# A fused attention, gated-convolution and axial-attention block on one core: the projection stored in four blocks, and three buffers for the local responses

## The chip, the cores and the metric

The kernel runs on one core of one Trainium2 chip. The metric is device time in microseconds (us) of one execution. The engines have short names throughout: PE is the matrix engine (PEld its weight load), DVE the vector engine, ACT the scalar engine, POOL the general-purpose engine, SP the engine that only issues transfers. SP's and POOL's transfers run on the same 16 DMA engines. L12 means line 12 of the kernel before.

## The reference, cut to what matters

Input and output are fp32 images of shape 4 x 64 x 256 x 256. Layer 0 works on them in this order:

```
xn   = channel_layernorm(x)
proj = conv1x1(xn, in_proj)                  # 64 channels
local, glob = proj[:, :32], proj[:, 32:]
local = gated 1x1 branch on local            # pre (1x1), a sigmoid response, a threshold = mean response
qkv  = depthwise3x3(conv1x1(glob))           # 96 channels
out  = top-k attention over channels (q, k, v), one small matrix per image
x    = x + conv1x1(concat(out, local), out_proj)
x    = x + gated convolution feed-forward(x) # 1x1 to 256 channels, depthwise 3x3 and 5x5, gelu gate, 8x8 FFT scaling
```

Layer 1 then does attention along rows, attention along columns and a feed-forward of width 256. Everything is fp32.

Two facts matter here. The response threshold needs the mean over the whole image, and the attention matrix needs sums over the whole image, so the projection has to be kept in DRAM and read again. And once an image's attention matrix is known, `v`, the attention, its scaling and the output projection collapse into one 3x3 convolution of `glob` to 64 channels, plus the local part.

## The kernel before

The work goes in five stages, each a Python loop that is fully unrolled. A scheduler places the recorded instructions: it fixes one order per engine ahead of time, and each engine then runs its own list in order and waits on semaphores. So an instruction that waits holds back everything behind it on its engine, needed or not.

**Stage A** (`stage_a`) goes over 4 images x 16 strips of 16 rows, 64 steps in all. `norm` normalises a strip. `proj` projects it to `pj`, 128 partitions of 2 branches x 2 row parities x 32 channels; partitions 0 to 63 are local and 64 to 127 global. `proj` ends with the stores of `pj` into `projd` in DRAM on POOL's queue, one per branch and parity (L551). Three steps behind, `pairs` builds the padded tile `gp` from `pj` by SBUF-to-SBUF transfers, clears its border columns on POOL (L569, L570), multiplies it into query/key tiles (L599), copies those out on DVE (`qT`, L604) and accumulates their Gram matrix (L590). For images 1 to 3, every second step also runs `local` for the image before: it reads `L4` from `projd` (L438), computes `pre` and a response `sw`, and stores them as `pred` and `resd`. After the loop, `local_last` does this for the last image while `attention_weights` makes the convolution weights `wc`.

**Stage C1** (`stage_c1`) goes over 32 strips of 8 rows x 2 pairs of images, 64 steps. `load` fetches, on SP's queue, `pre` (L718), `resp` (L719), two `gp` tiles (L725, L727, L729) and the input `xs` (L736). A `gp` tile here has 128 partitions: 32 global channels one row up, the same 32 unshifted, 32 local channels, and the 32 global ones one row down. The projection is stored once, so a tile takes three transfers:

```python
SY.dma_start(gp[32:96], pg[:, 8 * s:8 * s + 8])
SY.dma_start(gp[0:32, lo:8], pg[0:32, 8 * s - 1 + lo:8 * s + 7])
SY.dma_start(gp[96:128, 0:hi], pg[0:32, 8 * s + 1:8 * s + 1 + hi])
```

`front` turns the response into a mask in place (L743, then times `pre`, L744), runs the convolution in two halves of 24 matmul records each (L755) with the mask's matmul behind each half (L759), adds `xs` into `xm` (L765), transposes `xm` into `xmp` and normalises it. `back` transposes the normalised tile into `xl`. `hidden` makes the feed-forward's first 1x1 (L804), copies it out alternately on ACT (L810) and DVE (L808) into `tb`, and stores `tb` as `td` from POOL. All PSUM tiles of these steps rotate through six banks.

**Stage C2** does the depthwise convolutions, **C3** the FFT scaling and row attention, **D** the column attention and last feed-forward.

Of the kernel before, what the change touches and what calls it, by code (L numbers as in the profile page):

```python
# [9 lines left out]
F32 = mybir.dt.float32  # L10
# [4 lines left out]
C, H, W = 64, 256, 256  # L15
HW = H * W
# [231 lines left out]
def kernel(ctx: ExitStack, tc: tile.TileContext, x, packs, fd, out, off):  # L248
    nc = tc.nc
    B = x.shape[0]  # L250
    V, S, T, G, SY = nc.vector, nc.scalar, nc.tensor, nc.gpsimd, nc.sync
# [3 lines left out]
    dram = ctx.enter_context(tc.tile_pool(name="dram", bufs=1, space=bass.MemoryType.DRAM))  # L255

    def mm():
        return ps.tile([128, 512], F32, tag="mm", name="mm")
# [18 lines left out]
    V.memset(eps_t, EPS)  # L277


    projd = dram.tile([B, 64, H, W], F32, name="projd")  # L280


    NI, R0 = 9, 28
# [36 lines left out]
    p = sp1.enter_context(tc.tile_pool(name="pst", bufs=2))  # L320
# [113 lines left out]
    def local_load(b, i):  # L434
        l4 = p.tile([128, 8 * W], F32, name="L4")
        for k in range(4):
            r = 64 * k + 8 * i
            SY.dma_start(l4[k * 32:(k + 1) * 32], projd[b, 32:64, r:r + 8, :].rearrange("c u w -> c (u w)"))  # L438
        l4s[b, i] = l4

    def local_store(dst, b, i, src):
# [39 lines left out]
    def stage_a():  # L481
        NS = H // 16
        with tc.tile_pool(name="pa", bufs=2) as pa, tc.tile_pool(name="pa1", bufs=1) as pk:
# [4 lines left out]
            t = mm()  # L488
# [34 lines left out]
            def proj(b, s):  # L523

                pj = pa.tile([128, 8, W], F32, name="pj", bufs=4)
                pjs[b, s] = pj
                xn2 = xns.pop((b, s))
                xTs = []
                for hf in (0, 1):
                    xT = pa.tile([128, 1024], F32, name="xT")  # L530
                    for k in (0, 1):
                        tq = mm()
                        for i in range(4):
                            g = k * 8 + i * 2
                            T.transpose(tq[:, i * 128:(i + 1) * 128], xn2[hf][:, g:g + 2, :].rearrange("p a c -> p (a c)"), ident)
                        V.tensor_copy(xT[:, k * 512:(k + 1) * 512], tq)
                    xTs.append(xT)
                    yield
                for hf in (0, 1):
                    for k in (0, 1):  # L540
                        pr = mm()
                        T.matmul(pr, win, xTs[hf][:, k * 512:(k + 1) * 512], start=True, stop=True)
                        n = (s * 2 + hf) * 2 + k
                        S.activation(pj[:, hf * 4 + k * 2:hf * 4 + k * 2 + 2, :].rearrange("p a c -> p (a c)"), pr, AF.Identity,
                                     bias=bin_, accum_out=sacc[b][:, n:n + 1])
                    yield
                pv = projd[b, :, 16 * s:16 * s + 16, :].rearrange("(l c) (t a) w -> l a c t w", l=2, a=2)
                for lg in (0, 1):
                    for par in (0, 1):
                        q = lg * 64 + par * 32  # L550
                        G.dma_start(pv[1 - lg, par], pj[q:q + 32])  # L551
                hp = mm()
                for i in range(4):
                    T.matmul(hp[i * 32:(i + 1) * 32, :], K("g1T"), pj[:, 2 * i:2 * i + 2, :].rearrange("p a c -> p (a c)"), start=True, stop=True)
                hs = pa.tile([128, 512], F32, name="hs")
                V.tensor_scalar(hs, hp, K("g1b"), 0.0, ALU.add, ALU.max)
                hss[b, s] = hs
# [54 lines left out]
            for n in range(len(seq) + 3):  # L612
                if n + 1 < len(seq):
                    ld[seq[n + 1]] = load(*seq[n + 1])
                if 0 <= n - 2 < len(seq):
                    gate(*seq[n - 2])

                m = n - NS - 2
                lb, li = m // NS, m % NS
                if m >= 0 and lb < B - 1 and li % 2 == 0:  # L620
                    local_load(lb, li // 2)
                _steps(*(f(*seq[n - d]) for d, f in ((3, pairs), (1, proj), (0, norm)) if 0 <= n - d < len(seq)),
                       local(lb, li // 2) if m >= 0 and lb < B - 1 and li % 2 == 1 else None)
                if m >= 0 and lb < B - 1 and li == NS - 1:
                    local_end(lb)
                if n >= 1 and n - 1 < len(seq) and seq[n - 1][1] == NS - 1:
                    b = seq[n - 1][0]
                    V.tensor_reduce(sumA[:, b:b + 1], sacc[b], AX.X, ALU.add)
                    local_weights(b)
                if n >= 3 and seq[n - 3][1] == NS - 1:  # L630
                    b = seq[n - 3][0]
                    V.tensor_copy(gram2[b][0:64], grams[b][0:64, 0:64])
                    V.tensor_copy(gram2[b][64:128], grams[b][64:128, 64:128])
# [3 lines left out]
    def local_last():  # L637
        b = B - 1
        local_load(b, 0)
        for i in range(8):  # L640
            if i < 7:
                local_load(b, i + 1)
            yield from local(b, i)
        local_end(b)
# [49 lines left out]
    def stage_c1():  # L694
        NS = H // 8
        with ExitStack() as cs:
            p = cs.enter_context(tc.tile_pool(name="pc", bufs=2))
# [3 lines left out]
            t = mm()  # L701
# [6 lines left out]
            t = mm()  # L708
# [5 lines left out]

            def load(pr, s):
                pre = p.tile([128, 4 * W], F32, name="pre")
                resp = p.tile([128, 4 * W], F32, name="resp")
                SY.dma_start(pre, pred[pr, s].rearrange("h b c n -> (h b c) n"))  # L718
                SY.dma_start(resp, resd[pr, s].rearrange("h b c n -> (h b c) n"))  # L719
                gps = []  # L720
                for i in (0, 1):

                    gp = p.tile([128, 8, W], F32, tag="gp", name="gp", bufs=4)
                    pg = projd[2 * pr + i]
                    SY.dma_start(gp[32:96], pg[:, 8 * s:8 * s + 8])  # L725
                    lo = 1 if s == 0 else 0
                    SY.dma_start(gp[0:32, lo:8], pg[0:32, 8 * s - 1 + lo:8 * s + 7])  # L727
                    hi = 7 if s == NS - 1 else 8
                    SY.dma_start(gp[96:128, 0:hi], pg[0:32, 8 * s + 1:8 * s + 1 + hi])  # L729
                    if lo:  # L730
                        G.memset(gp[0:32, 0:1, :], 0.0)
                    if hi == 7:
                        G.memset(gp[96:128, 7:8, :], 0.0)
                    gps.append(gp)
                xs = p.tile([128, 8, W], F32, name="xs")
                SY.dma_start(xs, xf[pr * 128:(pr + 1) * 128, 8 * s:8 * s + 8])  # L736
                ld[pr, s] = xs, pre, resp, gps
# [93 lines left out]
            NP = B // 2  # L831
            seq = [(pr, s) for s in range(NS) for pr in range(NP)]
            load(*seq[0])


            for n in range(len(seq) + 3):
                if n + 1 < len(seq):
                    load(*seq[n + 1])
                _steps(after(back(*seq[n - 2]) if 1 < n < len(seq) + 2 else None, hidden((n - 3) // 2, (n - 3) % 2) if n > 2 else None),
                       front(*seq[n]) if n < len(seq) else None)  # L840
# [486 lines left out]
```

## Time and profile before

| what | value |
|---|---|
| three runs | 9669.94, 9681.12, 9686.45 us, median 9681.12 |
| the profiled execution's own time | 9679.41 us |
| its span, first to last instruction | 9677.6 us |
| PE, DVE, ACT, POOL busy, share of the span | 92%, 63%, 48%, 12% |
| DMA packets, bytes, mean rate | 1258452, 1831.36 MB, 189 GB/s |
| mean granted TensorE clock | 0.958 |
| stage A with the last local pass | about 0 to 1850 us |
| stage C1 | about 1850 to 3780 us |
| stages C2, C3, D | about 3780 to 5330, to 7310, to 9678 us |

In the views, a group or a row of the timeline gives line, engine, operation, tile written `<-` tiles read and a count, with the engine's idle time before it in brackets. A view of stretches gives, for each, the busy time of the five engines, then the granted clock, the mean busy share of the 16 DMA engines, and what they moved in GB/s. Matmuls are pipelined and their ends modelled, so PE's busy time is not a measure of PE at its peak.

### The profile page before, as it was taken

What the parts mean: (1) busy time and instruction counts of PE and PEld (TensorE: products, weight loads), DVE (VectorE), ACT (ScalarE), POOL (GpSimd) and SP (SyncE); (2) the same over time, 40 slices, a digit from 0 to 9 for tenths busy, and PEclk for the clock granted to TensorE, in tenths of its full rate; (3) what the DMA queues carried; (4) which work ended last, traced back from release to release, by engine and by line L of the source; (5) the groups of instructions that cost most, each with busy time, mean ns of one, the idle gap of its engine ahead of it and who ended that gap; (6) DMA issues with size and microseconds to landing.
All of it is one profiled execution on the core that took longest, in us unless ns stands there. A gap on an engine that the chain in (4) does not pass through costs nothing. (4 is left out here: it accounts for less than half of the span.)

```text
span 9677.6 us, 130500 instructions
## 1 busy us (share of the span) xinstructions
PE 8860.6 (92%) x51310; PEld 4971.4 (51%) x51310; DVE 6090.5 (63%) x8570; ACT 4599.0 (48%) x7332; POOL 1134.1 (12%) x1828
## 2 busy tenths in 40 slices
PE   8999999698888888999999999999998999899997
PEld 7877777344444443333333466666665444444443
DVE  6666665466666664222222588888886777777775
ACT  4455555444444443222222344444444666666665
POOL 0111111111111111000000011111110000000000
PEclk9999999799999999999999999999997999999998
DMA  6677776799999998888888644444432322322322
GB/s 146 143 174 176 169 172 163 220 344 333 340 332 334 338 341 307 298 297 298 297 296 297 202 142 143 148 145 144 147 107 52 70 61 44 70 61 47 68 61 44
DMA packets 1258452, 1831.36 MB, mean 189 GB/s; under 512 B 335600, under 2 KB 1040112, under 8 KB 1196656
## 3 DMA queue, kind: packets, MB, share of 16 engines
q1 hardware_dynamic: 1053296, 1034.32, 36.7%
q0 software_dynamic: 204544, 788.69, 24.7%
q8 instruction: 407, 6.67, 0.3%
q14 instruction: 205, 1.68, 0.1%
HBM read 967.34 MB, written 788.53 MB: 181 GB/s over the span
## 5 line engine op out<-in xcount | busy, mean ns | idle before, releaser
L895 DVE TENSOR_TENSOR y<-ge,mm 128x512 f32<-128x512 f32 (+1 forms) x640 | 406.0, 635 | 1225.8 <-ACT ge L894 1225.8
L862 PE MATMUL mm<-t,w 128*128 128x512 f32 (+1 forms) x2560 | 1094.1, 566 | 19.6 <-DMA t<-td 19.6
L894 ACT ACTIVATE ge<-mm 128x512 f32<-128x512 f32 (+1 forms) x640 | 354.6, 554 | 1253.8 <-PE mm L869 1253.8
L862 PEld LDWEIGHTS mm<-t,w 128*128 128x128 f32 x2560 | 456.3, 190 | 647.3 <-issue 437.0
L755 PE MATMUL mm<-gp,wc 128*64 128x510 f32 (+1 forms) x3072 | 701.9, 596 | 83.1 <-DVE xm L765 50.9
L1270 ACT ACTIVATE hg<-mm,b 128x512 f32<-128x512 f32 x1024 | 629.3, 687 | 299.6 <-PE mm L1268 298.1
L599 PEld LDWEIGHTS mm<-wqk,gp 128*128 128x128 f32 x6144 | 712.0, 192 | 71.2 <-issue 42.3
L599 PE MATMUL mm<-wqk,gp 128*128 128x128 f32 x6144 | 733.7, 276 | 0.0
L1279 PE MATMUL mm<-hg,pack_d 128*64 128x512 f32 x2048 | 590.9, 632 | 109.7 <-ACT hg L1270 109.7
L810 ACT COPY tb<-mm 128x512 f32<-128x512 f32 x512 | 299.8, 586 | 779.8 <-PE mm L804 779.7
L804 PE MATMUL mm<-xl,pack_c 64*128 64x512 f32 x2048 | 532.5, 617 | 132.7 <-DVE tb L808 127.7
L1268 PE MATMUL mm<-xfT,w 64*128 64x512 f32 x2048 | 621.4, 673 | 3.2 <-ACT xfT L1257 2.9
L869 PE MATMUL mm<-t,w 64*64 64x504 f32 (+1 forms) x5120 | 575.6, 556 | 0.0
L755 PEld LDWEIGHTS mm<-gp,wc 128*64 128x64 f32 x3072 | 277.1, 137 | 462.3 <-issue 331.2
L309 ACT ACTIVATE ln_sq<-xn 128x1024 f32<-128x1024 f32 x256 | 274.6, 1073 | 429.0 <-DVE xn L307 428.9
L1281 DVE TENSOR_SCALAR st<-mm,pack_d 128x512 f32<-128x512 f32 x256 | 278.8, 1089 | 212.6 <-PE mm L1279 212.6
L804 PEld LDWEIGHTS mm<-xl,pack_c 64*128 64x128 f32 x2048 | 216.2, 189 | 376.7 <-DVE tb L808 186.7
L311 DVE TENSOR_REDUCE ln_v<-ln_sq 128x16 f32<-128x1024 f32 x256 | 311.6, 1218 | 146.8 <-ACT ln_sq L309 146.8
L765 DVE SCALAR_TENSOR_TENSOR xm<-mm,bx,xs 128x256 f32<-128x256 f32 x512 | 212.2, 476 | 297.3 <-PE mm L759 297.3
L1146 ACT ACTIVATE ln_sq<-xc 128x1024 f32<-128x1024 f32 x256 | 268.8, 1057 | 224.6 <-DVE xc L1144 223.4
L1268 PEld LDWEIGHTS mm<-xfT,w 64*128 64x128 f32 x2048 | 219.2, 206 | 297.6 <-issue 146.9
L1147 DVE TENSOR_REDUCE v<-ln_sq 128x16 f32<-128x1024 f32 x256 | 307.2, 1211 | 91.7 <-ACT ln_sq L1146 91.6
(448 smaller groups left out, 16826.0 us busy)
## 6 DMA issues: line engine op xcount, KB each, us to landing
t<-td SPq DMA_DIRECT2D x256, 1152.0 KB, 10.0
td<-tb POOLq DMA_DIRECT2D x144, 1024.0 KB, 10.6
td<-tb POOLq DMA_DIRECT2D x288, 512.0 KB, 9.2
yd<-y POOLq DMA_DIRECT2D x128, 1152.0 KB, 10.1
ya<-yd SPq DMA_DIRECT2D x192, 512.0 KB, 5.8
xs<-in_x_dram SPq DMA_DIRECT2D x128, 512.0 KB, 6.7
projd<-pj POOLq DMA_DIRECT2D x256, 256.0 KB, 4.8
gp<-projd SPq DMA_DIRECT2D x128, 512.0 KB, 7.5
```

The source lines that it names most:

```text
L311: V.tensor_reduce(s2, sq, AX.X, ALU.add)
L599: T.matmul(qp[:, k * 128:(k + 1) * 128], gp[:, 2 * i + k // 2, at + dx:at + dx + 128], wqk[:, dx, :], start=(dx == 0), stop=(dx == 2))
L755: T.matmul(tv[i * 64:(i + 1) * 64, :, o], wc[2 * pr + i][:, dx, :], gps[i][:, 2 * r:2 * r + 2, i_], start=(dx == 1), stop=False, skip_grou ...
L804: T.matmul(t, inT[q, hf * 128:(hf + 1) * 128], xls[b // 2, s][q, :, 2 * y:2 * y + 2].rearrange("p f y t -> p f (y t)"), start=True, stop=True)
L862: T.matmul(t[:, :n], w[:, 0:128], x_[:, c, :], start=True, stop=False, skip_group_check=True)
L869: T.matmul(t[po:po + 64, :n].rearrange("p (n c) -> p n c", c=64)[:, :, o], w[q:q + 64, 128:192], x_[q:q + 64, c, i_], start=False, stop=Tr ...
L894: S.activation(ge[:, :n], ts[0][k][:, :n], AF.Gelu)
L895: V.tensor_tensor(y[:, c, :].rearrange("p n c -> p (n c)"), ge[:, :n], ts[1][k][:, :n], ALU.mult)
L1147: V.tensor_reduce(s2, sq, AX.X, ALU.add)
L1268: T.matmul(t, w1[rh * 64:(rh + 1) * 64, i * 128:(i + 1) * 128], xT[rh * 64:(rh + 1) * 64], start=True, stop=True)
L1270: S.activation(g, t, AF.Gelu, bias=b1[:, i:i + 1])
L1279: T.matmul(y[rh * 64:(rh + 1) * 64, :], w2[:, i, :], hg[i * 2 + rh], start=False, stop=(i == 1), skip_group_check=True)
```

## The change

The projection's DRAM tensor becomes four blocks of 32 channels: global one row down, global, local, global one row up. So each global strip is stored three times, shifted as the convolution's tile wants it, and stage A issues eight stores a step in place of four. Stage C1 then reads a `gp` tile in one transfer to 128 partitions (two for the first and the last strip). The `resp` tile gets three buffers instead of two. The order that the scheduler makes of the kernel changes with it.

```diff
-    projd = dram.tile([B, 64, H, W], F32, name="projd")
+    projd = dram.tile([B, 4, 32, H, W], F32, name="projd")
...
-            SY.dma_start(l4[k * 32:(k + 1) * 32], projd[b, 32:64, r:r + 8, :].rearrange("c u w -> c (u w)"))
+            SY.dma_start(l4[k * 32:(k + 1) * 32], projd[b, 2, :, r:r + 8, :].rearrange("c u w -> c (u w)"))
...
-                pv = projd[b, :, 16 * s:16 * s + 16, :].rearrange("(l c) (t a) w -> l a c t w", l=2, a=2)
-                for lg in (0, 1):
+                for blk, shift, q in ((1, 0, 64), (2, 0, 0), (0, 1, 64), (3, -1, 64)):
                     for par in (0, 1):
-                        q = lg * 64 + par * 32
-                        G.dma_start(pv[1 - lg, par], pj[q:q + 32])
+                        y0 = 16 * s + par + shift
+                        t0, t1 = int(y0 < 0), 8 - int(y0 + 14 >= H)
+                        dst = bass.AP(tensor=projd.tensor, offset=projd[b, blk, 0, y0 + 2 * t0].offset, ap=[[HW, 32], [2 * W, t1 - t0], [1, W]])
+                        G.dma_start(dst, pj[q + par * 32:q + par * 32 + 32, t0:t1])
...
-                resp = p.tile([128, 4 * W], F32, name="resp")
+                resp = p.tile([128, 4 * W], F32, name="resp", bufs=3)
...
-                    pg = projd[2 * pr + i]
-                    SY.dma_start(gp[32:96], pg[:, 8 * s:8 * s + 8])
-                    lo = 1 if s == 0 else 0
-                    SY.dma_start(gp[0:32, lo:8], pg[0:32, 8 * s - 1 + lo:8 * s + 7])
-                    hi = 7 if s == NS - 1 else 8
-                    SY.dma_start(gp[96:128, 0:hi], pg[0:32, 8 * s + 1:8 * s + 1 + hi])
-                    if lo:
+                    pg = projd[2 * pr + i].rearrange("j c y w -> (j c) y w")[:, 8 * s:8 * s + 8]
+                    if s == 0:
                         G.memset(gp[0:32, 0:1, :], 0.0)
-                    if hi == 7:
+                        SY.dma_start(gp[0:32, 1:8], pg[0:32, 1:8])
+                        SY.dma_start(gp[32:128], pg[32:128])
+                    elif s == NS - 1:
                         G.memset(gp[96:128, 7:8, :], 0.0)
+                        SY.dma_start(gp[0:96], pg[0:96])
+                        SY.dma_start(gp[96:128, 0:7], pg[96:128, 0:7])
+                    else:
+                        SY.dma_start(gp, pg)
```

What the scheduler's order of each engine looks like after the change, against before:

- POOL in stage A: before, four stores and one pair of `gp` border clears alternate; after, sixteen stores (two steps) and then two pairs of clears.
- DVE in stage A: in every second step the copies of the first query/key tile and of the second `xT` (L604, L536) stand behind the layernorm's last reciprocal and multiply (L315, L316); before they stood ahead of them.
- SP in stage C1, per step: before `pre`, `gp`, `resp`, five more `gp`, `xs`; after `resp`, `pre`, `gp`, `gp`, `xs`.
- DVE in stage C1: the mask's first instruction (L743) stood between two `tb` copies of the same step; after, it stands behind all `tb` copies of the step and behind the first half's layernorm subtract, and the eight `xm` instructions are interleaved with the layernorm instead of standing four by four.
- PE: the same order as before, apart from C1's first steps.

## The prediction

> **What bounds the kernel now.** I read the page's slices first, then stretches by stage, then the waits and one step's timeline in each stage that the change touches.
>
> ```profile
> PE   8999999698888888999999999999998999899997
> DVE  6666665466666664222222588888886777777775
> DMA  6677776799999998888888644444432322322322
> ```
>
> A slice is 242 us. Stage A is slices 1 to 7: PE full, DMA at 6 to 7 tenths. Stage C1 is slices 9 to 15: DMA at 9 tenths and PE just short of full.
>
> ```profile
> 0.00:1740.00 1740.00, 1648.22 (x13004) 1304.91 (x13004) 1084.31 (x1310) 925.03 (x1574) 266.12 (x589) 0.97 0.68 162
> 2000.00:3660.00 1660.00, 1428.37 (x6684) 697.05 (x6682) 1122.91 (x1560) 774.63 (x1339) 308.18 (x441) 0.96 0.93 338
> ```
>
> Stage A: PE busy 95%, DMA 0.68. C1: PE 86%, DMA 0.93 at 338 GB/s. The issues of `xs` (L736) repeat every 29.8 us on average in C1 (first eight steps aside), so 54 steady steps. What holds such a step is in the waits of 1990 to 3700 us:
>
> ```profile
> DVE resp L743 <- DMA resp<-resd: 187.1, 57, 6.8
> PE mm L804 <- DVE tb L808: 127.7, 56, 5.8
> SPq L725 <- PE mm L755: 1071.8, 56, 25.0
> ```
>
> and in one step, where the convolution ends at 2526.0:
>
> ```profile
> 2526.06 0.49 SPq L725 DMA_DIRECT2D gp<-projd  x1
> 2527.19 0.32 SPq L719 DMA_DIRECT2D resp<-resd  x1
> 2530.21 0.36 SPq L736 DMA_DIRECT2D xs<-in_x_dram  x1
> 2532.30 1.28 DVE L743 SCALAR_TENSOR_TENSOR resp<-resp,thr 128x1024 f32<-128x1024 f32 x1 [2.29 <-DMA resp<-resd]
> 2533.50 0.68 DVE L808 COPY tb<-mm 128x512 f32<-128x512 f32 x1
> 2534.24 1.13 PE L804 MATMUL mm<-xl,pack_c 64*128 64x512 f32 x4 [1.24 <-DVE tb L808]
> ```
>
> With two buffers, `resp` of the step after next can be fetched only when this step's mask matmul (L759) is done. DVE's fixed order asks for it 5 us later, and the `tb` copies that PE needs stand behind it. That mask is used more than a step later: the wait is one of order, 187.1/57 = 3.3 us a step.
>
> The other limit is the DMA rate, which depends on what is moved:
>
> ```profile
> 1860.00:1864.00 4.00, 1.72 (x2) 0.52 (x3) 0.00 (x0) 0.00 (x0) 0.00 (x0) 0.50 0.95 201
> 2532.00:2534.00 2.00, 0.99 (x4) 0.16 (x4) 1.70 (x2) 1.20 (x3) 0.00 (x0) 1.00 0.97 238
> 2544.00:2552.00 8.00, 7.13 (x34) 2.73 (x32) 6.16 (x10) 4.17 (x8) 0.12 (x1) 1.00 1.03 419
> ```
>
> All three have the engines full. 201 and 238 GB/s are in the `gp` loads, two thirds of whose transfers touch 32 partitions; 419 is 128-partition stores and `xs`.
>
> [...] The trace's two rates are used below. [...]
>
> **Part 1: one read of `gp`.** Bytes stay 1 MB a tile. Of 2 MB a step, 1 MB goes in 32-partition transfers: at 210 GB/s 5.0 us, at 420 2.5 us. Saving 2.5 us of DMA time a step. The step now has 0.93 x 29.8 = 27.7 us of DMA, then 25.2. By itself this moves no end; it sets when loads land. SP's nine issues a step become five, each 0.3 to 0.6 us, which SP has time for. The first eight steps, with few `td` stores, run at the pace of their reads (14.5 to 26.6 us between `xs` issues): about 15 us saved, 5 to 25.
>
> **Part 2: `resp` and the new order in C1.** `resp` no longer waits for this step's L759, but SP's queue puts it behind two `gp` and `xs`. `xs` waits for `xm`, 2.8 us after the convolution's end (t0), so `resp` is issued at t0+3.2 with 3 MB ahead. I walk a step with the trace's durations. From t0 DVE does four `xm` (to 2.8), two `tb`, two `tb`, layernorm sum (behind `xmp`, 6.4 to 7.6), `tb`, subtract, `tb`: to 10.2. Then the mask wants `resp`. Behind it stand sum of squares 1.2, sum 1.2, reciprocal 0.25, subtract 1.2, multiply 1.2, L744 1.2, sum of squares 1.2: with the mask's 1.3 that is 8.8 until the first `xm`. Two `xm` and a reciprocal (1.1) free the first bank for the second half of the convolution, 5.4 long. A step is thus max(landing, 10.2) + 15.3. The same walk with the old order (landing at 7.0, then 22.1 of DVE and PE) gives 29.1 where 29.8 is measured, so I add 0.7.
>
> The landing: before, `xs` closes the same 3.5 MB; it is issued at t0+4.2 and lands a median 13.1 later, 17.3. That is about 1.5 of latency and 10.9 of transfer at the two rates (1 MB at 210), so stores took some 4.9 us. Now the transfer is 8.3: 3.5 before the next `td` store is issued, 4.8 against it. At a share of 60 to 70% for the reads in that part, 12 to 13; I take 12.5. Step: 12.5 + 15.3 + 0.7 = 28.5. Saved 1.3 x 54 = 70 us. Bounds: landing at 10.2, 26.2, which DMA's 25.2 allows only at 96%; I take 26.9, saving 157. Landing at 15, 31.0, costing 65.
>
> **Part 3: four more stores a step in stage A.** 256 KB each from 32 partitions; at about 210 GB/s 1 MB is 5 us of DMA. A step is 1740/64 = 27.2 us with 18.5 of DMA; it becomes 23.5, 0.86. PE hides it: loads there are issued 12 to 25 us ahead of use. Without that cover it would be 5 x 64 = 320. On POOL the stores take 0.58 us each (2.31 for four), 4.6 instead of 2.3. Queued behind are the clears of `gp`, on which PE's L599 waits. In a step without `local` they end at 264.73+4.8 = 269.5; L599 starts at 271.97. With `local`: 987.1 against 990.91. Covered by 2.4 and 3.8.
>
> **Part 4: DVE's order in stage A.** Half of the pair steps put `qT` and `xT` behind the layernorm's end. With `local`, 24 times: `qT` moves from 995.28 to 997.9, since the reciprocal waits for ACT's root (996.00+0.31) and the multiply takes 1.22. A matmul that started at 996.02 waits for that bank: PE is 2.6 late. Downstream, where PE idled 2.2 for `qT` at 1015.52, half is absorbed; following ACT's chain I get 1.3 left. Without `local`, 6 times: the Gram matmul at 254.68 waits for a `qT` that ends at 257.0, 2.3, nothing absorbed. Sum 31 + 14 = 45 us. Bounds 15 (more absorbed) and 80 (none).
>
> **Sum.** -15 - 70 + 45 = -40. Against the span, 9677.6 - 40 = 9637.6; the median of runs stands 3.5 above the span: 9641.
>
> **Rivals.**
>
> *A, `resp` is never late.* If reads win over stores, the landing comes by 10.2 and C1 goes to 26.9 a step: -157 - 15 + 45 = -127, 9554. For it: DMA's load falls, so fewer stores are queued at t0. Against: 3.5 MB at 420 plus latency is 9.8 with no store at all.
>
> *B, the wait comes back larger (slower).* DVE's wait on `resp` at L743 now ends with the last transfer of the burst. If it lands at 15.0, a step is 31.0: +65 - 15 + 45 = +95, 9776. It decides from 13.2 on, where C1's gain, 0.6 x 54 + 15, is just the 45 lost in stage A. For it: `xs` landed at 15.3 to 19.4 before. Against: those carry the slow megabyte.
>
> *C, stage A pays more.* The clears or `gp` rows come late, 4 us in 30 steps, or part 4 at its top: another +80 to +120, so about 9740.
>
> *D, nothing to be seen.* The losses and gains cancel, or the slow rate comes from rereading the same DRAM rows and not from 32 partitions, with the buffer's gain paying for stage A: 9681. This is also the case in which the single read does not do what it says.
>
> **Chances.** Forecast 0.40, A 0.16, B 0.24, C 0.12, D 0.08. A change under 0.2% (19 us) can't be told from none here. The forecast's own spread, 9590 to 9690, is 0.30 faster, 0.08 same, 0.02 slower; A all faster; B all slower; C 0.10 slower, 0.02 same; D 0.02, 0.04, 0.02. Sums: 0.48, 0.14, 0.38. The range is 9540 to 9770: A and B are in but for their ends. The forecast's own range stands beside it, 9590 to 9690.
>
> **What would show it.** Right: `gp`'s landing shorter and C1 above 345 GB/s while its DMA share falls or stays; 28 to 29 us between `xs` issues; DVE still waiting about 2 to 3 us a step on `resp`, now behind the subtract; stage A 45 us longer with PE waiting on `qT`. Wrong: no such wait left (A), a wait over 5 us (B), L599 waiting on POOL (C), `gp` windows still near 240 GB/s (D). A stage A unchanged in length would refute part 4.

## The result and the profile after

The changed kernel takes 9812.7 us in the median of its four runs (9808.8 to 9816.0), the kernel before 9681.7 us in runs on the same chip. The ratio is 1.0137 (95% interval 1.0119 to 1.0155): slower by 1.4%. The forecast was 9641 us, and its range ended at 9770. The profiled execution's span is 9814.2 us, 136.6 more than before.

Line numbers move with the change: before's L743 (mask) is L746 here, L744 is L747, L755 and L759 (the convolution and the mask's matmul) are L758 and L762, L765 (`xm`) is L768, L804 is L807, L808 is L811.

The page's slices of DMA:

```profile
DMA  8788888788888888888888744444442222332322
```

Stage A's DMA went from 6 to 7 tenths to mostly 8 (the four more stores), and C1's from 9 to 8. The same two stretches as before, stage A and C1:

```profile
0.00:1740.00 1740.00, 1619.65 (x12477) 1291.86 (x12478) 1073.90 (x1271) 920.93 (x1546) 402.73 (x823) 0.96 0.85 196
2000.00:3660.00 1660.00, 1467.58 (x6418) 626.51 (x6416) 1069.61 (x1496) 736.67 (x1283) 291.96 (x418) 0.92 0.83 322
```

In C1 the DMA share fell from 0.93 to 0.83, but the rate fell too, from 338 to 322 GB/s, since the same bytes took longer. DMA has more room and the stage is slower: it waits. The granted TensorE clock fell from 0.96 to 0.92.

From the issue times of transfers, the 136.6 us are: stage A and the last local pass +59.8 (the first `xs` of C1 is issued at 1915.5 us instead of 1855.8), C1 +82.4 (from its first to its last `xs` 1892.9 us instead of 1810.5), and the stages behind it -5.6. The steady step of C1 is 31.2 us instead of 29.9.

The waits of 1990 to 3700 us, as before (total, times, longest):

```profile
DVE resp L746 <- DMA resp<-resd: 256.5, 55, 8.4
...
PE mm L758 <- DVE xm L768: 125.0, 55, 2.4
```

DVE's wait on the responses, which the third buffer should ease, grew from 3.3 to 4.7 us a step. PE no longer waits for DVE's `tb`; it waits for `xm`, which now stands behind the mask (125.0 us in this stretch; 49.2 before). One step of the timeline, where the convolution ends (t0) at 2616.9:

```profile
2609.13 7.79 PE L758 MATMUL mm<-gp,wc 128*64 128x512 f32 x24 [2.43 <-DVE xm L768]
...
2616.94 0.80 SPq L736 DMA_DIRECT2D gp<-projd  x2
...
2620.13 0.40 SPq L721 DMA_DIRECT2D resp<-resd  x1
...
2621.39 0.75 POOL L825 DMA_DIRECT2D td<-tb  x1 [8.01 <-ACT tb L813]
...
2623.03 1.50 POOL L825 DMA_DIRECT2D td<-tb  x2 [0.88 <-ACT xmp L780]
...
2631.47 1.28 DVE L746 SCALAR_TENSOR_TENSOR resp<-resp,thr 128x1024 f32<-128x1024 f32 x1 [4.42 <-DMA resp<-resd]
```

The responses are issued at t0+3.2, as forecast, and the mask starts at t0+14.5. Two `td` stores are issued at t0+4.5 and t0+6.1. In the step of the kernel before that the prediction shows (t0 at 2526.0), the second came only at t0+10.4:

```profile
2530.53 0.75 POOL L822 DMA_DIRECT2D td<-tb  x1 [6.72 <-ACT tb L810]
...
2536.44 1.50 POOL L822 DMA_DIRECT2D td<-tb  x2 [5.16 <-ACT tb L810]
```

The DMA in the same burst of the changed kernel, from the view of stretches (the last two columns are the share and GB/s):

```profile
2620.00:2622.00 2.00, 2.00 (x11) 0.89 (x9) 1.75 (x4) 1.46 (x3) 0.60 (x1) 1.00 1.00 422
...
2624.00:2626.00 2.00, 2.00 (x16) 1.36 (x13) 2.00 (x3) 1.06 (x2) 0.52 (x1) 1.00 0.96 291
2626.00:2628.00 2.00, 1.70 (x14) 1.22 (x12) 1.05 (x2) 1.16 (x2) 0.42 (x1) 1.00 0.97 373
```

The reads now run at 422 where the three-piece reads ran at 200 to 240: the single read does what it says. The two stretches behind it are slower with the engines just as full. In the first of them only SP's queue (q1: packets, MB, share of 16 engines) moved anything, so it is reads alone that are slow there:

```profile
q1 hardware_dynamic: 72, 0.58, 95.7%
```

POOL's store of 2621.39 moves its first packet at 2626.0, 4.6 us after its issue.

Rival D of the prediction put the old slow rate down to rereading the same DRAM rows. One place speaks against that. In C1's first strip the changed kernel reads each tile in two transfers, to 32 and to 96 partitions, and no row twice; it is slow there too:

```profile
1918.00:1925.00 7.00, 2.72 (x4) 0.88 (x5) 2.51 (x2) 0.00 (x0) 0.00 (x0) 0.50 1.01 256
```

No run changes the rereading alone, and none the number of partitions alone: that a transfer to 32 partitions is what is slow is an estimate of the prediction's, from its rows of 201 and 238 GB/s against 419.

### The profile page after: what moved, and what is told of

It reads as the page before. It is cut to its first block, busy times and chain, and to the rows that moved or that the text cites. A ratio compares the mean times of both kernels' runs of the same rounds, so it can differ in the third digit from the quotient of the medians.

```text
span 9814.2 us, 130424 instructions
## 1 busy us (share of the span) xinstructions
PE 8990.8 (92%) x51310; PEld 4955.8 (50%) x51310; DVE 6091.8 (62%) x8570; ACT 4606.0 (47%) x7332; POOL 1280.3 (13%) x2084
## 3 DMA queue, kind: packets, MB, share of 16 engines
q0 software_dynamic: 225024, 855.56, 27.5%
## 5 line engine op out<-in xcount | busy, mean ns | idle before, releaser
L758 PE MATMUL mm<-gp,wc 128*64 128x510 f32 (+1 forms) x3072 | 789.6, 666 | 174.5 <-DVE xm L768 133.1
L601 PEld LDWEIGHTS mm<-wqk,gp 128*128 128x128 f32 x6144 | 754.2, 201 | 91.3 <-issue 35.1
L601 PE MATMUL mm<-wqk,gp 128*128 128x128 f32 x6144 | 776.2, 286 | 14.9 <-POOL gp L580 14.9
L807 PE MATMUL mm<-xl,pack_c 64*128 64x512 f32 x2048 | 592.9, 615 | 56.6 <-ACT xl L795 56.2
L758 PEld LDWEIGHTS mm<-gp,wc 128*64 128x64 f32 x3072 | 253.7, 153 | 673.3 <-issue 625.6
L768 DVE SCALAR_TENSOR_TENSOR xm<-mm,bx,xs 128x256 f32<-128x256 f32 x512 | 221.9, 467 | 324.4 <-PE mm L762 324.4
L553 POOL DMA_DIRECT2D projd<-pj x512 | 295.7, 585 | 965.3 <-ACT ln_d L314 755.2
L807 PEld LDWEIGHTS mm<-xl,pack_c 64*128 64x128 f32 x2048 | 236.7, 188 | 343.5 <-ACT xl L795 153.8
```

The lines of the kernel that those rows point to most:

```text
L601: T.matmul(qp[:, k * 128:(k + 1) * 128], gp[:, 2 * i + k // 2, at + dx:at + dx + 128], wqk[:, dx, :], start=(dx == 0), stop=(dx == 2))
L758: T.matmul(tv[i * 64:(i + 1) * 64, :, o], wc[2 * pr + i][:, dx, :], gps[i][:, 2 * r:2 * r + 2, i_], start=(dx == 1), stop=False, skip_grou ...
L807: T.matmul(t, inT[q, hf * 128:(hf + 1) * 128], xls[b // 2, s][q, :, 2 * y:2 * y + 2].rearrange("p f y t -> p f (y t)"), start=True, stop=True)
```

## The experiments

Two theories were set against each other. "Order": the loss of C1 comes from where the responses' fetch and the mask now stand in SP's and DVE's lists. "Burst": reading `gp` in one piece crowds reads against stores, whatever the order. Times are medians of four runs; each ratio is against the kernel before on the same chip.

**Two buffers again.** Undoes the third buffer alone.

```diff
-                resp = p.tile([128, 4 * W], F32, name="resp", bufs=3)
+                resp = p.tile([128, 4 * W], F32, name="resp")
```

> The changed kernel with two buffers for the responses again; the stores and the single read of gp stay. DVE's order in C1 is then that of the kernel before (mask between the tb copies), and on SP the responses' fetch stands behind one gp read instead of behind both and xs. Theory 'order': the loss in C1 comes from the fetch's and the mask's new places, so this kernel loses it: steady step 28.5 us (28 to 29.5) against 31.2 in the changed kernel, DVE's wait on the responses about 2 us a step and PE's wait on tb back. Stage A keeps its 60 us. Total 9700 us (9670 to 9730). Rival 'burst': reading gp in one piece crowds the reads against the td stores whatever the order; then the step stays at 30.5 us or more and the total at 9770 us or more.

Measured: 9756.1 us, ratio 1.0085 (1.0070 to 1.0100). Stage A keeps its loss (+55.5 at the first `xs`), and C1's steady step is 30.1 us. That lies between the two theories' numbers: better than the changed kernel, no better than before. The waits and the stretch 2000 to 3400 us:

```profile
DVE resp L746 <- DMA resp<-resd: 161.2, 46, 7.1
...
PE mm L807 <- DVE tb L811: 115.5, 47, 6.1
```

```profile
2000.00:3400.00 1400.00, 1199.46 (x5594) 557.70 (x5596) 941.83 (x1309) 649.18 (x1121) 252.61 (x361) 0.95 0.86 333
```

DMA works 0.86 x 30.1 = 25.9 us a step instead of 27.8, so the single read saves 1.9 us of DMA (2.5 forecast). The step doesn't feel it: the mask starts at t0+7.5 (before 7.3), with the responses behind a `gp` of 1 MB instead of 0.5 MB, and 22.6 us follow it in both kernels.

**The third buffer alone**, in the kernel before.

```diff
-                resp = p.tile([128, 4 * W], F32, name="resp")
+                resp = p.tile([128, 4 * W], F32, name="resp", bufs=3)
```

> The kernel before with a third buffer for the responses and nothing else. SP's order in C1 is unchanged (responses ahead of gp), and on DVE the mask moves up by one tb copy. Theory 'order': the buffer by itself brings nothing, since the mask is put as early as a free buffer lets it and so still asks for data fetched in the same step: step 29.5 to 30.5 us, total 9681 us within 30. Rival 'buffer': a third buffer takes the wait away wherever the reads stand, so the step falls by the 3.3 us of the wait, total about 9500 us; or the buffer itself is what costs, and the step goes to 31 us, total about 9750 us.

Measured: 9444.6 us, ratio 0.9762 (0.9748 to 0.9777), and a steady step of 25.8 us. The theory as I had put it ("the buffer by itself brings nothing") fell; the rival came near. The stretch and one step, with t0 at 2608.5:

```profile
2000.00:3400.00 1400.00, 1328.73 (x6534) 641.00 (x6534) 1109.19 (x1523) 758.95 (x1310) 297.29 (x424) 1.00 1.01 389
```

```profile
2604.71 1.28 DVE L743 SCALAR_TENSOR_TENSOR resp<-resp,thr 128x1024 f32<-128x1024 f32 x1 [0.33 <-DMA resp<-resd]
...
2614.60 0.34 SPq L719 DMA_DIRECT2D resp<-resd  x1
```

The responses are issued late, at t0+6.1, behind `gp` and `xs`. But the mask stands 7 us later than in the changed kernel, at t0+22, behind the first four `xm` of the next convolution, where DVE would idle for PE's second half. On average it starts 15.8 us after the issue, just when the data has landed (a median 15.6 us after the issue), and of `tb` and the layernorm only one `tb` copy stands between it and the next `xm`. So a third buffer is worth 225 us in C1 if the mask stands there. The changed kernel has the buffer and the mask in another place. From here on the theory is "place".

**The mask's place alone.** Two kernels keep the changed kernel's loads and stores and tie the mask of step n+2 in DVE's list behind an `xm` of step n: behind the last one (first kernel), and behind the first four (second kernel, "in the gap"). The tie fixes the order and adds no wait.

```diff
-                V.scalar_tensor_tensor(mk, resp, thr[pr], resp, ALU.is_gt, ALU.max)
+                m = V.scalar_tensor_tensor(mk, resp, thr[pr], resp, ALU.is_gt, ALU.max)
+                if (pr, s - 1) in last_xm:
+                    tc.add_manual_dep(m.ins, last_xm[pr, s - 1].ins.name, mybir.DependencyInfo(mybir.DependencyClass.NoSync, mybir.DependencyReason.DATA), reason="order")
...
```

> The changed kernel, but the mask of step n+2 is tied (in order only, no wait) behind the last xm of step n on DVE, so it uses responses that were fetched a whole step earlier. Loads and stores as in the changed kernel. Theory 'order': DVE's wait on the responses goes from 4.6 us a step to under 0.5, the steady step from 31.2 to 27 us (26.2 to 28), C1 loses 160 to 250 us; total 9590 us (9550 to 9650). The half-speed TensorE clock after PE's idle stretch goes with the idle. Rival 'burst': the reads and stores of a step are the bound and another load (xs or gp) becomes the last one: step 30 us or more, total 9760 us or more.

> The changed kernel with the mask of step n+2 tied in DVE's order behind the first four xm of step n, where DVE waits for PE's second half of the convolution. It is the place that the mask has in the kernel before with a third buffer. Theory 'place': as there, the mask runs in DVE's idle gap on data fetched a step before; with gp in one piece DMA has slack too, so the steady step is 25 us (24.5 to 25.8), total 9475 us (9450 to 9510). Rival: the mask's place makes no more difference once its data is a step old, and the step stays at the 26.7 us of the kernel with the mask behind the last xm; total 9560 us.

Measured: behind the last `xm` 9561.1 us, ratio 0.9882 (0.9867 to 0.9897), step 26.7; in the gap 9494.3 us, ratio 0.9810 (0.9796 to 0.9825), step 25.7. Both are in the ranges of "order" and "place". The mean granted clock of the two executions is 0.962 and 0.961, that of the changed kernel's 0.949. In the first, no wait on the responses is left in 2000 to 3400 us; what is left is DVE's idle time before the second four `xm`, which the mask doesn't use:

```profile
2607.74 1.66 DVE L770 SCALAR_TENSOR_TENSOR xm<-mm,bx,xs 128x256 f32<-128x256 f32 x4 [4.62 <-PE mm L764]
...
2609.31 1.27 DVE L746 SCALAR_TENSOR_TENSOR resp<-resp,thr 128x1024 f32<-128x1024 f32 x1
```

In the second, the mask fills that time, 17.6 us after its data was issued, and waits for the responses 0.6 us in all:

```profile
2591.98 0.52 SPq L721 DMA_DIRECT2D resp<-resd  x1
...
2609.60 1.28 DVE L746 SCALAR_TENSOR_TENSOR resp<-resp,thr 128x1024 f32<-128x1024 f32 x1
```

```profile
DVE resp L746 <- DMA resp<-resd: 0.6, 3, 0.2
```

SP's order per step is that of the changed kernel, the bytes are the same, and 5.5 us a step have come back. "Burst" is out: with the same reads and stores C1 moves 390 GB/s at a share of 0.98:

```profile
2000.00:3400.00 1400.00, 1324.59 (x6558) 603.32 (x6554) 1109.80 (x1529) 762.27 (x1316) 296.83 (x424) 1.00 0.98 390
```

**Three reads again.** Undoes the single read alone; the eight stores and the third buffer stay.

```diff
-                        SY.dma_start(gp, pg)
...
+                    SY.dma_start(gp[32:96], pg[1:3, :, 8 * s:8 * s + 8].rearrange("j c y w -> (j c) y w"))
...
+                    SY.dma_start(gp[0:32, lo:8], pg[1, :, 8 * s - 1 + lo:8 * s + 7])
...
+                    SY.dma_start(gp[96:128, 0:hi], pg[1, :, 8 * s + 1:8 * s + 1 + hi])
```

> The changed kernel with its eight stores and its third buffer, but gp read as before in three pieces (from the two unshifted copies): only the single read is undone. DVE's order in C1 is then that of the kernel before with a third buffer (mask in the gap behind the first four xm). Theory 'place': C1 goes to that kernel's step of 25.8 us, stage A keeps its 60 us: total 9445 + 60 = 9505 us (9490 to 9525), 300 us faster than the changed kernel although its reads are the slower ones. Rival 'stores': something in the new layout costs C1 as well (copies of one row lie 8 MB apart), and the step stays at 27 us or more, total 9570 us or more.

Measured: 9501.6 us, ratio 0.9820 (0.9803 to 0.9836), step 25.8, first `xs` at 1915.7: as "place" said, to 4 us. The slower reads make a kernel that is 311 us faster, because with them the order puts the mask back into the gap.

**`xs` behind the responses.** `xs` is loaded a step later in program order, so that on SP the responses come ahead of it.

```diff
-                ld[pr, s] = xs, pre, resp, gps
+                ld[pr, s] = pre, resp, gps
...
-                xs, pre, resp, gps = ld.pop((pr, s))
+                xs = load_x(pr, s)
+                pre, resp, gps = ld.pop((pr, s))
```

> The changed kernel, but xs of a step is loaded after the next step's responses: on SP the responses' fetch now stands behind two gp reads only, and xs follows. DVE's order stays of the new kind (mask after the tb copies and before the end of the layernorm; one copy and one sum earlier than in the changed kernel). Theory 'landing': the step is the landing of the responses plus what follows the mask, about 16 to 18 us; without 1 MB ahead they are issued 2 us earlier and land at about t0+10 instead of t0+14.5, so the steady step is 27 to 28.5 us, total about 9630 us (9590 to 9680). Rival 'burst': the whole burst of 3.5 MB and the td stores bound the step, whatever is last in it: 30 us or more, total 9760 us or more.

Measured: 9811.2 us, ratio 1.0141 (1.0126 to 1.0156), step 31.1. The landing did what was expected, and the step didn't. Here t0 is 2592.5:

```profile
2593.63 0.32 SPq L721 DMA_DIRECT2D resp<-resd  x1
...
2602.08 1.28 DVE L750 SCALAR_TENSOR_TENSOR resp<-resp,thr 128x1024 f32<-128x1024 f32 x1 [4.00 <-DMA resp<-resd]
...
2603.28 1.21 DVE L307 TENSOR_REDUCE ln_s<-xmp 128x16 f32<-128x1024 f32 x1
...
2622.75 0.82 SPq L736 DMA_DIRECT2D gp<-projd  x2
```

The mask starts at t0+9.5, five earlier. But it has moved up too, ahead of the layernorm's first sum, and 20.7 us now follow it instead of 16.2. My "16 to 18" for what follows was the error. The rival's numbers (30 us or more, 9760 or more) came true, but its reason is out by the kernel with the mask in the gap. The means over 27 to 34 steps between 2400 and 3300 us say it for all kernels. They are in us, and "then" is from the mask to the next t0. Here t0 is the issue of the step's first `gp`; in the third buffer alone and the three reads it comes 0.8 and 1.0 us after the convolution's end, in the others with it:

| kernel | responses issued | mask starts | then | step |
|---|---|---|---|---|
| before | t0+1.1 | t0+7.3 | 22.6 | 29.9 |
| two buffers | t0+1.1 | t0+7.5 | 22.6 | 30.1 |
| changed | t0+3.2 | t0+14.9 | 16.2 | 31.1 |
| `xs` behind | t0+1.2 | t0+9.8 | 21.4 | 31.2 |
| third buffer alone | t0+6.3 | t0+22.1 | 3.7 | 25.8 |
| mask in the gap | t0+3.2 | t0+20.9 | 4.8 | 25.7 |
| three reads, third buffer | t0+6.6 | t0+22.2 | 3.6 | 25.8 |

In the first four rows DVE stands waiting for a transfer issued 6 to 12 us before, and a later landing comes with less work behind it. In the last three the mask is late enough to wait little: 1.3, 0.0 and 1.6 us a step, against 3.3 to 4.9 in the first four.

**Stage A: the border columns cleared once**, in two fixed buffers, so no column clear stands behind the eight stores.

```diff
-                gp = pa.tile([128, 8, W + 2], F32, name="gp")
-                G.memset(gp[:, :, 0:1], 0.0)
-                G.memset(gp[:, :, W + 1:W + 2], 0.0)
+                gp = gpa[s % 2]
...
+            gpa = [pa.tile([128, 8, W + 2], F32, name=f"gp{k}", bufs=1) for k in (0, 1)]
...
```

> The changed kernel, but in stage A the two zero columns of gp are cleared once in two fixed buffers instead of in every step on POOL, so no clear stands behind the eight stores; DVE's order in stage A is then that of the kernel before (qT and xT ahead of the layernorm's end). Theory 'DVE order': stage A's 60 us are the late qT and xT, and 40 to 60 of them come back: total 9760 us (9750 to 9775), C1 unchanged at 31.2 a step. Rival 'stores': they come from the four more stores (DMA share 0.87) and stay: total 9800 us or more.

Measured: 9766.1 us (9752.9 to 9784.9), ratio 1.0089 (1.0073 to 1.0106). DVE's order in the steps within an image is that of before again. The table goes by each image's first `gp` transfer: image 0 up to image 1's, images 1 to 3 up to the one of the last strip. In brackets stand PE's idle time and the granted clock of the stretch.

| kernel | image 0 | images 1 to 3 | first `xs` of C1 |
|---|---|---|---|
| before | 374.2 us (7.7; 0.99) | 1285.6 us (58.3; 0.97) | 1855.8 |
| changed | 399.6 us (21.3; 0.97) | 1322.3 us (78.3; 0.96) | 1915.5 |
| columns cleared once | 370.9 us (7.7; 1.00) | 1310.5 us (73.2; 0.97) | 1883.3 |

(The last row's trace is the slowest of its four runs, 19 us above their median: by the medians 47 us came back, as expected, and in the trace 32. So the split is good to some 20 us.) In image 0 all eight stores are issued each step and nothing is lost: the steps are 23.5 us as before, where the changed kernel alternates 23.5 and up to 27.5. So there the stores are hidden, and the loss is DVE's order. Of its 25 us PE idles 14, all of it for `qT`; in the rest PE is busy longer, at a lower granted clock.

In images 1 to 3 only 12 of 37 us came back in the trace. PE's waits in 100 to 1700 us, of the kernel before, the changed one and this one:

```profile
PE sm L590 <- DVE qT L604: 50.4, 23, 2.2
```

```profile
PE mm L458 <- DVE qT L606: 51.4, 19, 2.7
PE sm L592 <- DVE qT L606: 18.7, 10, 2.0
PE mm L601 <- POOL gp L580: 14.9, 3, 5.0
```

```profile
PE sm L590 <- DVE qT L604: 58.3, 26, 5.9
```

With the smaller of the two waits for `qT` (5.0 before, 3.9 here) the sums are 55, 70 and 62 us. So late `qT` isn't the whole loss. In the changed kernel PE also waits, once at each change of image, for the clear of the first strip's outer row. POOL's new order, sixteen stores and then two pairs of clears, holds in image 0 only: in images 1 to 3 the second pair stands behind the `pred` stores, and at a change of image the row's clear stands behind the first of these, which waits for ACT:

```profile
470.19 0.56 POOL L444 DMA_DIRECT2D pred<-pre  x1 [7.87 <-ACT pre L462]
470.75 0.33 POOL L580 MEMSET gp<- 32x258 f32 x1
```

With the columns cleared once, no matmul of stage A waits for a clear. What stays sits at the changes of image: two steps there take 38.3 and 31.3 us, before 32.1 and 27.2, and the longest wait for `qT` (5.9 us) is there. Between them a pair of steps takes 55.0 us as before (54.9).

**Both repairs, and the row clears.** The mask in the gap together with the columns cleared once; then also the clears of the first and last strip's outer row on DVE instead of POOL.

```diff
-                    G.memset(gp[0:32, 0:1, :], 0.0)
+                    V.memset(gp[0:32, 0:1, :], 0.0)
...
-                    G.memset(gp[96:128, 7:8, :], 0.0)
+                    V.memset(gp[96:128, 7:8, :], 0.0)
```

> The kernel with the mask in the gap, and in stage A the zero columns of gp cleared once in two fixed buffers. If the parts add up, the sum of both gains: about 40 us under the kernel with the mask in the gap, 9435 us (9410 to 9470), about the same as the kernel before with only a third buffer (9445 us). If they do not, as much as that kernel alone.

> As the kernel with the mask in the gap and the columns cleared once, with the two row clears of each image (first and last strip) on DVE instead of POOL, where they stand behind eight stores. Theory 'clears behind stores': what is left of stage A's loss sits at the three image changes (12 us each in the kernel with the columns cleared once, and none between them), and 20 to 35 us of it come back: about 9410 us. Rival: the waits there have another cause, and nothing changes (9435 us).

Measured: both repairs 9457.3 us, ratio 0.9778 (0.9761 to 0.9794), a sum as expected. With the row clears on DVE 9509.5 us, ratio 0.9828 (0.9814 to 0.9843): the expectation was wrong. The clears themselves are few, but DVE's list was made anew, and from the end of image 1 on a pair of steps takes 35.3 + 23.5 = 58.8 us instead of 55.0. Why `qT` is late at the changes of image stays open.

The best kernel is thus the simplest: the kernel before with the third buffer alone, 9444.6 us. The kernel with both repairs can't be told from it (the intervals overlap), so the new layout has no gain left to show: in the traces it is 11 us faster in C1 (1573.8 against 1585.1 us from first to last `xs`), and its first `xs` comes 20 us later.

**PE's slow halves.** In the changed kernel 24 of the 58 halves of the convolution that begin between 2400 and 3300 us took 6.7 to 8.3 us instead of 5.36 (the expectations below have another count, 22 of 55). The granted clock (the column before the DMA share) shows why:

```profile
2606.00:2608.00 2.00, 0.70 (x4) 0.00 (x0) 2.00 (x3) 0.37 (x1) 0.00 (x0) 0.81 0.13 41
2608.00:2610.00 2.00, 0.87 (x2) 0.33 (x4) 2.00 (x5) 1.27 (x3) 0.00 (x0) 0.50 0.73 258
...
2612.00:2614.00 2.00, 2.00 (x6) 0.53 (x4) 0.10 (x1) 0.00 (x0) 0.75 (x1) 0.50 0.02 10
```

Two kernels put matmuls that nobody reads into PE's idle stretch ahead of the second half, five or two a step, with every other order kept.

```diff
+                    if ra and last_h:
+                        w = sm()
+                        for _ in range(5):
+                            d = T.matmul(w, ident, gps[0][:, 0:2, :], start=True, stop=True)
...
```

> The changed kernel with five more matmuls a step (128x512, into a bank that nobody reads) ahead of the second half of the convolution, where PE stands idle for 2.4 us until xm; every engine's order stays as it was. In the changed kernel 22 of 55 halves of the convolution ran at half the granted clock for a while (6.7 to 8.3 us instead of 5.36), 1.6 us a step on average. Theory 'idle': the halving comes from PE's idle stretch and lies on the path, so with the stretch filled the halves take 5.36 us and the steady step falls from 31.2 to about 29.7 us, total about 9730 us (9715 to 9770). Rival 'no part of the path': the slow halves are covered by the wait on the responses, or the fillers cost what they bring: step 30.8 us or more, total 9790 us or more.

> The kernel with fillers ahead of the second half of the convolution, with two of them instead of five. Five took 4.56 us where PE idles 2.4: the slow halves were gone (0 of 56) but the half began 2.1 us later, and the step stayed at 31.2 us. Two take 1.8 us and fit. Theory 'idle on the path': halves at 5.36 us and no later start, the step falls to about 29.7 us, total about 9735 us (9715 to 9770). Rival 'no part of the path, or the clock falls again': with only part of the stretch filled the step stays at 30.8 us or more, total 9790 us or more.

Measured: five fillers 9826.9 us, ratio 1.0156 (1.0141 to 1.0171); two 9801.6 us, ratio 1.0126 (1.0109 to 1.0143). One step of each, five first (the trace counts each of these matmuls twice):

```profile
2609.49 4.56 PE L755 MATMUL sm<-gp,pack_k 128*128 128x512 f32 x10
2613.98 5.36 PE L763 MATMUL mm<-gp,wc 128*64 128x512 f32 x24
```

```profile
2610.84 1.98 PE L755 MATMUL sm<-gp,pack_k 128*128 128x512 f32 x4
...
2613.36 5.36 PE L763 MATMUL mm<-gp,wc 128*64 128x512 f32 x24 [0.53 <-DVE xm L773]
```

In both no half took over 5.9 us (0 of 58): PE's idle time ahead of the half is what makes it slow. The mean granted clock of 2000 to 3660 us is 0.92 in the changed kernel, 0.96 with two fillers and 0.99 with five (over the whole execution 0.949, 0.954 and 0.961), so with two the clock still falls in some steps, but no half pays for it. In time it brought little, and the rival's numbers came true twice. Five fillers took as much as they gave. With two, what follows the mask fell from 16.2 to 15.4 us, but the mask started 0.7 us later, and the step fell by only 0.3. So of the expected 1.5 us 0.8 was there to be had, and most of that was given back in the landing; why the landing moves isn't shown.

## Why the prediction was wrong

**Part 1, the single read: near in size, and right that it moves no end by itself.** DMA time fell by 1.9 us a step (2.5 taken), pure reads went to about 420 GB/s, and with two buffers the step didn't shorten. The start of C1 failed: its first eight steps take 179 us instead of 167, where 15 less were taken. The first five are 7 us faster, then the new wait sets in.

**Part 2, the third buffer: the failed step is the landing, "I take 12.5".** The mask starts at t0+14.9, 2.4 later, and 2.4 x 54 = 130 us is most of the distance between the 28.5 us step and the measured 31.2. The terms of that sum, counted over the same 27 steps by the packets of SP's and POOL's queues:

- The reads are 3.67 million bytes. The walk divided 3.5 by 420 GB/s; it is 8.7 us, not 8.3.
- The latency, 1.5, was an estimate, and it is near. The first packet of `gp` moves a median 0.95 us after its issue, and the responses land a median 0.53 us after SP's last packet of data.
- By t0+4.5, when the first store is issued, 1.03 MB of the reads had moved. The walk had 3.5 us at 420 GB/s, 1.47 MB. Reads run at that rate only from t0+3 on, and 0.36 MB of stores left over from the step before moved in the same time.
- The other 2.64 MB took 10.4 us, where 2.0 MB in 7.4 us was walked. The reads' share wasn't the error: 66% of what moved was theirs, and 60 to 70% was taken. But it was 66% of 385 GB/s, not of 420.

The step shown above has the same shape, with 386 GB/s behind the first store's issue. From t0 to that issue, and from there to the landing (q1 is SP's queue, q0 POOL's):

```profile
q1 hardware_dynamic: 155, 1.16, 76.2%
```

```profile
q1 hardware_dynamic: 421, 2.51, 67.1%
q0 software_dynamic: 345, 1.35, 32.7%
```

A smaller part is a transfer that came early. The step that the working predicts removes PE's wait for `tb`, so the `tb` copies come earlier, and in the steps shown the second store with them, by 4.3 us. I moved the copies and not the transfers that they release. Of the 1.36 MB of stores behind t0+4.5 the first store is 1.05, so at most 0.3 MB is the second's: about 0.8 us at 385 GB/s, an estimate.

What follows the mask came out right, 16.2 us against 15.3 + 0.7, but in part by luck. The 0.7 was carried over from the old order's miss; here the slow halves of the convolution fill it, which the walk didn't have. With two fillers, 15.4 us follow.

**The larger omission** is that the third buffer's value was read from this one order. Alone it saves 231 us; with the single read it costs. The prediction took the two edits as one sum (-15, -70) and didn't ask what the buffer is worth in the order that it would have without the other edit.

**Rival B was right**, in mechanism, step (31.0 against 31.2 us) and sign; only its mark, a wait over 5 us, wasn't quite reached (4.7). Its 9776 lacks 37 us: the start of C1 (+12 instead of -15, so 27) and stage A (15), less the 6 that the later stages gained.

**Part 3, hidden: right for the stores, wrong for one clear.** With the eight stores the DMA share of 0 to 1740 us went from 0.68 to 0.85 (0.86 taken). Eight stores cost nothing in image 0 once DVE's order is restored. But PE waits for a clear on POOL three times (14.9 us in all), once at each change of image. That is rival C's mark. The covers of 2.4 and 3.8 us were read inside an image, with the clears straight behind the stores, and not at a change of image.

**Part 4, DVE's order in stage A: shown in image 0 only; 45 taken and 60 measured, and the nearness is in part luck.** Image 0 lost 25 us against 14: six steps at 2.3 were counted, and its late steps cost up to 4. Images 1 to 3 lost 37 us against 31. Of these, 20 are PE's idle time: 15 the wait for the clear, 4 more of waiting for `qT`. In the rest PE is busy longer at a granted clock of 0.96 instead of 0.97. The working had neither term, and with DVE's old order only 12 of the 37 came back in the trace.

## What to carry to other kernels

In a kernel whose engine lists are made ahead of time, an extra buffer is not slack; it is leave to move the consumer, and where it then stands decides. Ask for each wait how long before it the transfer was issued, and put the consumer where the engine idles anyway: here two edits, one nearly neutral in C1 by itself and the other worth 225 us there, made a loss of 82 us together, and one order tie was worth 318 us. When a step moves, walk the transfers too: those that it releases, and those that the step before has left in the queues.

## What the runs showed of the hardware

In the changed kernel the clock fell to half without one long idle stretch. The row of 2606 to 2608 us has a mean of 0.81. In quarters of a microsecond the clock is 0.99 in 2607.00 to 2607.25 and 0.50 in 2607.25 to 2607.50, so the fall comes at about 2607.2. PE had been idle for only 0.5 us then (from 2606.7). In the 4.8 us from 2602.4 to the fall it worked 2.3 us, in two short pieces, and its longest idle stretch was 1.1 us. The idle stretch in which the clock fell went on to 2.43 us in all, and the clock stood at 0.50 until about 2614 (0.50 in 2613.5 to 2614, 0.96 in the microsecond behind it). What sets the moment of the fall isn't shown.

The reads of a burst didn't run at a steady rate, with the engines full: from t0+3 to the landing their busy share is 0.96 to 1.05 in each us. In the means over the 27 steps they move 410 to 421 GB/s from t0+3 to t0+7, then 337 and 289 in the next two us, still with hardly a packet of a store beside them. The stores' packets join at about t0+9, and the two together move 364 to 414. Why the reads slow down isn't shown.
